# Values on every other partition, maxima turned by VectorE, and half tiles in the second layer's first pass

## The chip, the cores and the metric

The kernel runs on one core of a Trainium2 chip. The metric is device time in microseconds (us) from start to end of one execution; lower is better. A core has five engines that work side by side, each through its own list of instructions: TensorE (PE, matrix products), VectorE (DVE), ScalarE (ACT), GpSimd (POOL) and SyncE (SP, which here issues nearly all DMA transfers). They work on SBUF, a memory of 128 partitions (rows); TensorE writes its sums into PSUM, eight banks of 2 KB a partition (512 fp32 numbers). DRAM is reached by DMA only.

## The reference

Two layers on B = 2 sequences of T = 2048 tokens with D = 256 features, all fp32. Each layer normalizes x, runs an attention and a gate on the result, and adds their product.

```python
def attn0(x):                       # full attention, 16 heads of 16 features
    q, k, v = split(x @ w_qkv.T + b_qkv)
    p = softmax(q @ k.T / sqrt(256))
    return (p @ v) @ w_o.T + b_o + x
def attn1(x):                       # local attention: only keys with |i - j| <= 64
    q, k, v = x @ w_qkv + b_qkv
    p = softmax(q @ k.T * 16**-0.5 + band)
    return (p @ v) @ w_out + b_out
for attn, ffn in ((attn0, ffn0), (attn1, ffn1)):
    xn = layernorm(x)
    x = x + attn(xn) * silu(ffn(xn))
```

ffn0 mixes 8 experts of 64 features with a running sum over the sequence, ffn1 is a linear layer with 8 low-rank experts. The change doesn't touch them.

## The kernel before

Everything lies with features on partitions and tokens along the row (`x`, `xn`, `gt`: [128, 2, 2048] per sequence). The stages follow each other: weights and first norm; ffn0; `attention` for layer 0; second norm and ffn1; `attention` again with `local=True`.

**Heads in row groups.** `attention` keeps the queries and keys of four heads at a time in tiles `qs[.]`, `ks[.]`: head j of the group in partitions 32j to 32j+31 (`hp`, L548), of which 16 hold values. A matmul of one head uses 32 rows of the array, so four heads fill the four row groups. `keys_queries` (L473) projects and writes to the DRAM tensor `qd` [2, B, H, 32, T]; `fetch` (L581) brings 32 rows a head back. Rows 16 to 31 of `qd` were preset with ones (keys) and zeros (queries) by DMA (L304 to L311). Row 16 of the queries later gets minus the query's largest score, so that the product with the ones subtracts it. Two sets of `qs`, `ks` alternate.

**Items and steps.** An item is (sequence, group of four heads, block of 512 queries): 32 of them. A step of layer 0 is one block of 128 keys against the item's 512 queries (U = 16 steps an item); a step of layer 1 is two query blocks of 128 with the keys in their reach (U = 2). The main loop (L945) runs, per step s:

- `scores` (L596): TensorE computes two things. The **second pass** (`sk`) has keys as weights and queries as columns, for step s; ACT takes its exponential (L683), and in layer 1 GpSimd puts zeros outside the band (`affine_select`, L688). The **first pass** (`sq`) has queries as weights, for a step U + LEAD later; it serves only to find the maxima, by VectorE: in layer 0 a `tensor_reduce` (L679), in layer 1 `tensor_tensor_reduce` with a mask, eight a step (L674). Matmuls of both passes go out sorted by a number `when` (L666), which sends row groups 0, 1 through sk then sq and row groups 2, 3 the other way round.
- `weigh` (L733), DEL steps later: `acc` <- exponentials times values, one 32-column group per head (L747). The values `vs` hold 17 columns a head, the last all ones, so row 16 of each group of `acc` becomes the softmax's denominator. ACT copies `acc` to `av`.
- what `at(step, ...)` has booked for the step (L855 to L881): LEAD steps before an item begins, its maxima are turned from a column into a row; after the item, a chain with one hop or so a step divides and projects.

**Turning the maxima.** Layer 0 (`turn_max`, `fetch_max`): VectorE scales, SP writes element by element to DRAM (`md`), and three steps later reads it into `q` row 16. Layer 1 (`place_max`, L714): TensorE transposes (`pmx`, L720), ACT copies (L723), a DMA from ACT's queue puts the row in `q` (L726).

**The chain after an item** (L771 to L803), in layer 1 at hops 0, 1, 3, 4, 5, 7, 8: `away` writes `av` (128 x 512) to DRAM; `compact` reads the denominators back as [128, 16] (`dn`) and the values into `xn`; `invert` takes reciprocals; `write` puts them in DRAM; `spread` reads them broadcast over the head's rows (`recb`); `divide` multiplies (in layer 1 VectorE and GpSimd in turn); `project` (group 3 only) applies the output weights. The last four items of layer 1 go through TensorE instead (`last_there`, `last_back`).

**What sets the order.** A scheduler places instructions; those in `pin` keep their program order on their engine, so SP's transfers run in the order in which they are written. `values` (L526) projects the values, 17 blocks a sequence in layer 1, and VectorE or ACT copies them to `vs`, which GpSimd has set to ones before (L514).

Of the kernel before, what the change touches and what calls it, by code (L numbers as in the profile page):

```python
# [17 lines left out]
P = 128  # L18
# [6 lines left out]
HV = HD + 1  # L25
TB = 512
# [11 lines left out]
def two_layers(ctx: ExitStack, tc: tile.TileContext, a, out):  # L38
# [144 lines left out]
    def softmax8(pool, lg, groups, name):  # L183
# [12 lines left out]
        [2, B, H, HP, T], F32, name="qd"  # L196
# [3 lines left out]
    with tc.tile_pool(name="fw", bufs=1) as fw:  # L200
# [102 lines left out]

        zeros = fw.tile([P, TB], F32, name="zeros")  # L304
        nc.vector.memset(zeros, 0.0)
        for b in range(B):
            for i, t in ((0, ones), (1, zeros)):
                for half in range(NC):
                    nc.sync.dma_start(
                        out=qd[i, b, bass.ts(half, H // NC), HD:, :], in_=t[:, None, :].to_broadcast([P, NB, TB])  # L310
                    )  # L311
# [161 lines left out]
    def keys_queries(A, b, n, i, hf, bank, place):  # L473
        w, bias = ((A["k"], A["bk"]), (A["q"], A["bq"]))[i]
        ps = bank()
        for c in range(NC):
            nc.tensor.matmul(  # L477
                ps, w[:, c, bass.ts(hf, P)], xn[b][:, c, bass.ts(n, TB)], start=(c == 0), stop=(c == NC - 1)
            )
        sb = place()  # L480
        nc.scalar.activation(sb, ps, AF.Identity, bias=bias[:, hf : hf + 1])
        nc.sync.dma_start(out=qd[i, b, bass.ts(hf, H // NC), :HD, bass.ts(n, TB)], in_=sb)

    def attention(A, scale, local, final, start=None, projected=False):
# [16 lines left out]
        LEAD = 3 if local else 6  # L501
        DEL = 2 if local else 1
        with ExitStack() as st:
# [6 lines left out]
            ad = [dr.tile([NG, HP, TB], F32, name=f"ad{i}", tag=f"ad{i}") for i in range(3)]  # L510
            rd = [dr.tile([NG, TB], F32, name=f"rd{i}", tag=f"rd{i}") for i in range(3)]

            md = [dr.tile([NG * TT, P], F32, name=f"md{i}", tag=f"md{i}") for i in range(2)]
# [12 lines left out]
            def values(b, c, bank, copy):  # L526
                lo = c * P - PAD
                t0, t1 = max(lo, 0), min(lo + P, T)
                p0, p1 = t0 - lo, t1 - lo
                ps = bank()[:, :D]  # L530
                for dc in range(NC):
                    nc.tensor.matmul(  # L532
                        ps[p0:p1, :], xn[b][:, dc, t0:t1], A["v"][:, dc, :], start=(dc == 0), stop=(dc == NC - 1)
                    )
                copy(
                    vs[b][p0:p1, c, : H * HV].rearrange("p (h w) -> p h w", w=HV)[:, :, :HD],
                    ps[p0:p1, :].rearrange("p (h w) -> p h w", w=HD),
                )
# [10 lines left out]
            hp = [slice(j * HP, (j + 1) * HP) for j in range(NG)]  # L549
            ep = None if local else pool("ep", 8)  # L550
# [3 lines left out]
            if local:  # L554

                mask = mp.tile([P, 2 * P], F32, name="mask", bufs=1)
                nc.vector.memset(mask, 0.0)
                nc.gpsimd.affine_select(
                    out=mask, in_=mask, compare_op=ALU.is_ge, fill=MASKED, base=0,
# [3 lines left out]
                    out=mask, in_=mask, compare_op=ALU.is_ge, fill=MASKED, base=P,  # L563
                    pattern=[[-1, 2 * P]], channel_multiplier=1,
                )

# [14 lines left out]
            def fetch(bg, lo=0, hi=T):  # L581

                if bg >= B * NG:
                    return
                b, g = divmod(bg, NG)
                k0, k1 = max(lo - PAD, 0), (T if hi == T else hi - PAD)
                for i, t in ((1, qs[bg % 2]), (0, ks[bg % 2])):
                    to, s = (slice(lo, hi), slice(lo, hi)) if i else (slice(PAD + k0, PAD + k1), slice(k0, k1))
                    nc.sync.dma_start(out=t[:, to], in_=qd[i, b, bass.ts(g, NG), :, s].rearrange("h w t -> (h w) t"))
# [6 lines left out]
            def scores(second, first, es):  # L596
# [7 lines left out]
                if second:  # L604
# [3 lines left out]
                    if local:  # L608

                        qt = n * TT + 2 * u  # L610
                        segs = [
                            (P, 3 * P, bass.ts(qt + 1, P), bass.ds(qt * P, 2 * P)),
                            (0, P, bass.ts(qt, P), bass.ts(qt, P)),
                            (3 * P, 4 * P, bass.ts(qt + 2, P), bass.ts(qt + 1, P)),
                        ]
                    else:
                        segs = [(0, TB, bass.ts(u, P), bass.ts(n, TB))]
# [8 lines left out]
                    for j in range(NG):  # L626
# [6 lines left out]
                        when = 2 * (j // 2) if apart else 0  # L633
                        for lo, hi, ks_, qs_ in segs:
                            pieces.append((when, t[:, lo:hi], k[hp[j], ks_], q[hp[j], qs_]))
                            when += 2 * (hi - lo) / TB
                        tasks.append((es[j], t))
                pairs = []
                if first:
# [9 lines left out]
                    for pair in ((2, 3), (0, 1)):  # L649
                        sq = pmax.tile([P, 2, TB], F32, name="sq", tag="sq")  # L650
                        pairs.append((pair, sq))
                        for d, j in enumerate(pair):
                            when = (2, 2, 0, 0)[j] if apart else 0
                            if local:
                                for t in range(2):
                                    qt, lo, hi = reach(n1, u1, t)
                                    pieces.append((
                                        when + t, sq[:, d, t * 2 * P + lo : t * 2 * P + hi],
                                        q1[hp[j], bass.ts(qt, P)], k1[hp[j], qt * P + lo : qt * P + hi],
                                    ))  # L660
                            else:
                                t, kb = divmod(u1, NB)
                                pieces.append((
                                    when, sq[:, d], q1[hp[j], bass.ds(n1 * TB + t * P, P)], k1[hp[j], bass.ts(kb, TB)]
# [3 lines left out]
                for pair, sq in pairs:  # L668
                    if local:
                        for d, j in enumerate(pair):  # L670
                            for t in range(2):
                                qt, lo, hi = reach(n1, u1, t)
                                seen = mp.tile([P, 2 * P], F32, name="seen", tag="seen")
                                nc.vector.tensor_tensor_reduce(  # L674
                                    seen[:, lo:hi], sq[:, d, t * 2 * P + lo : t * 2 * P + hi], mask[:, lo:hi],
# [17 lines left out]
            def reach(n, u, t):  # L693

                qt = n * TT + 2 * u + t
                return qt, (PAD if qt == 0 else 0), (2 * P - PAD if qt == NT - 1 else 2 * P)

            pin = tc.keep_in_program_order

            def turn_max(i):  # L700

                mx, _ = part.pop(i)
                nmx = mp.tile([P, NG * TT], F32, name="nmx", tag="nmx")
                pin(nc.vector.tensor_scalar(nmx, mx.rearrange("p j t -> p (j t)"), -1.0, None, ALU.mult))
                pin(nc.sync.dma_start(out=md[i % 2].rearrange("j p -> p j"), in_=nmx))

            def fetch_max(i):

                pin(nc.sync.dma_start(
                    out=tiles(i)[0][HD:P:HP, bass.ts(items[i][2], TB)],  # L710
                    in_=md[i % 2].rearrange("(j t) p -> j (t p)", t=TT),
                ))

            def place_max(i):  # L714

                b, g, n = items[i]
                q = tiles(i)[0]
                mx, _ = part.pop(i)
                ps = pm.tile([NG * TT, P], F32, name="pmx", tag="m")
                nc.tensor.transpose(ps, mx.rearrange("p j t -> p (j t)"), ident)  # L720
                row = mp.tile([NG * TT, P], F32, name="row", tag="row", bufs=2 if local else 1)
                if local:
                    pin(nc.scalar.activation(row, ps, AF.Copy, scale=-1.0))  # L723
                else:
                    nc.vector.tensor_scalar(row, ps, -1.0, None, ALU.mult)
                pin((nc.scalar if local else nc.sync).dma_start(  # L726
                    out=q[HD:P:HP, bass.ts(n, TB)].rearrange("j (t c) -> j t c", c=P), in_=row
# [37 lines left out]

# [5 lines left out]
            def away(i):  # L771

                pin(nc.sync.dma_start(out=ad[i % 3].rearrange("j w f -> (j w) f"), in_=avs.pop(i)))

            def flat(d):

                return d.rearrange("j (r e) -> r j e", r=P // NG)

            def compact(i):

                divs[i] = op.tile([P, NG * TB // P], F32, name="dn", tag="dn", bufs=3)
                pin(nc.sync.dma_start(out=divs[i], in_=flat(ad[i % 3][:, HD, :])))
                pin(nc.sync.dma_start(out=together(*items[i]), in_=ad[i % 3][:, :HD, :].rearrange("j d f -> d j f")))
# [7 lines left out]
            def spread(i):  # L791
# [4 lines left out]
                pin(nc.sync.dma_start(out=divs[i], in_=rd[i % 3][None, :, :].to_broadcast([HD, NG, TB])))  # L796
# [8 lines left out]
            def last_there(i):  # L805
# [3 lines left out]
                for t in range(TT):  # L809
                    nc.tensor.transpose(ps[:, t].rearrange("p j w -> p (j w)"), av[:, bass.ts(t, P)], ident)  # L810
                rec = op.tile([P, TT, NG], F32, name="dn", tag="dn", bufs=3)
                o = divs[i] = op.tile([P, TT, HD, NG], F32, name="over", tag="recb", bufs=2)
                nc.vector.reciprocal(rec, ps[:, :, :, HD])
                nc.vector.tensor_tensor(
                    o.rearrange("p t d j -> p t j d"), ps[:, :, :, :HD],
                    rec[:, :, :, None].to_broadcast([P, TT, NG, HD]), ALU.mult,
                )

            def last_back(i):
# [3 lines left out]
                o = divs.pop(i).rearrange("p t d j -> p t (d j)")  # L823
# [35 lines left out]
            for i, (b, g, n) in enumerate(items):  # L859
                if local:  # L860
                    at(i * U - LEAD, place_max, i)
                else:
                    at(i * U - LEAD, turn_max, i)
                    at(i * U - LEAD + 3, fetch_max, i)
# [257 lines left out]
def _attn_arrays(l, wq, wk, wv, bq, bk, bv, wo_t, bo):  # L1122

    apart = lambda m: m.reshape(NG, NG, HD, -1).transpose(0, 2, 1, 3).reshape(m.shape)
# [5 lines left out]
        f"wo{l}": apart(np.asarray(wo_t).T),  # L1130
        f"bq{l}": cols(bq),
        f"bk{l}": cols(bk),
        f"bv{l}": cols(apart(np.asarray(bv))),
# [56 lines left out]
```

## Time and profile before

| | |
|---|---|
| median of 3 runs | 2535.94 us (2533.43 to 2537.54) |
| the profiled execution, its span | 2538.34 us, 2536.6 us |
| 0 to 470: weights, norm, ffn0 | PE busy 461.8 |
| 470 to 597: layer 0's projections and first steps | PE busy 124.7 |
| 597 to 2111: layer 0's attention, 512 steps | PE busy 1513.9 of 1514 |
| 2111 to 2225: norm and ffn1 | PE busy 110.0 of 114 |
| 2225 to 2292: layer 1's projections and first steps | PE busy 66.2 of 67 |
| 2292 to 2537: layer 1's attention, 64 steps and the end | PE busy 236.5 of 245 |

TensorE's granted clock is 0.999 over the span. In the rows of a stretch or of single instructions that follow, PE is the matmuls and PEld the loading of their weights, which runs beside them. A matmul row names its output and inputs, the tile of the array that it uses (32*128: 32 rows, 128 columns), and the columns that flow through it. Times are in us from the start of the span; the number before the engine is the duration.

### The profile page before, as it was taken

How to read it: one execution, taken by the hardware profiler on the slowest of the kernel's cores; microseconds unless marked ns; L12 is line 12 of the kernel's file. 1: busy time of each engine (PE TensorE's matmuls, PEld its weight loads, DVE VectorE, ACT ScalarE, POOL GpSimd, SP SyncE). 2: the span in 40 equal slices, each digit the busy share in tenths (PEclk: the TensorE clock that was granted, in tenths of full speed). 3: DMA queues.
4: the chain of work that ended last, by engine and by line, in shares of the span. 5: the costliest groups of instructions: out<-in, count | busy, mean ns of one | idle time of the engine just before them, and what ended most of it. 6: DMA issues, size and time to landing. Idle time of an engine off the chain costs nothing.

```text
span 2536.6 us, 47898 instructions
## 1 busy us (share of the span) xinstructions
PE 2513.1 (99%) x18896; PEld 1060.6 (42%) x18896; DVE 1686.2 (66%) x2747; ACT 1620.8 (64%) x3187; POOL 876.6 (35%) x827
## 2 busy tenths in 40 slices
PE   8999999999999999999999999999999999999999
PEld 6444444444333333333333333333333334457766
DVE  4143333157888888888777788788888765238986
ACT  5400000126888888888888888888888886227755
POOL 0000000102444444444444444444444420016887
PEclk9999999999999999999999999999999999999999
DMA  6131111230001001001001001001000002133552
GB/s 243 50 84 51 52 51 39 82 118 14 14 14 43 16 12 44 16 12 44 16 12 43 10 18 44 12 17 43 15 14 10 14 14 63 49 133 108 163 167 81
DMA packets 146353, 129.83 MB, mean 51 GB/s; under 512 B 93456, under 2 KB 97936, under 8 KB 143568
## 3 DMA queue, kind: packets, MB, share of 16 engines
q1 hardware_dynamic: 144256, 125.46, 16.5%
q8 instruction: 148, 2.42, 0.4%
q10 hardware_dynamic: 1872, 1.31, 0.2%
q14 instruction: 77, 0.63, 0.1%
HBM read 80.50 MB, written 45.97 MB: 50 GB/s over the span
## 4 chain that ended last, share of the span: by engine, by line
PE 79%; DMA 1%; ACT 0%; POOL 0%; DVE 0%; issue 0%; ACTq 0%; SPq 0%; POOLq 0%; DVEq 0%
PE sk L667 25%; PE acc L747 22%; PE sq L667 19%; PE pp L477 5%; PE pr L835 2%; PE pp L532 2%; PE po L1027 1%; PE pt L1023 1%; PE po L1035 1%; PE xb L113 0%; PE xb L138 0%; DMA k<-qd 0%; PE of L827 0%; DMA q<-qd 0%; POOL xn L688 0%
## 5 line engine op out<-in xcount | busy, mean ns | idle before, releaser
L679 DVE TENSOR_REDUCE part<-sq 128x2 f32<-128x1024 f32 x1024 | 1207.3, 1221 | 294.3 <-PE sq L667 284.7
L683 ACT ACTIVATE e<-sk 128x512 f32<-128x512 f32 x2048 | 1058.3, 603 | 217.2 <-PE sq L667 197.7
L667 PE MATMUL sk<-q,k 32*128 32x512 f32 (+2 forms) x5632 | 1135.8, 533 | 1.2 <-ACT xn L683 1.0
L667 PE MATMUL sq<-k,q 32*128 32x512 f32 (+2 forms) x5120 | 1129.1, 569 | 0.5 <-DVE part L679 0.5
L761 POOL TENSOR_TENSOR av<-av,more 128x512 f32<-128x512 f32 x459 | 581.4, 1267 | 936.3 <-ACT more L760 931.1
L667 PEld LDWEIGHTS sk<-q,k 32*128 32x128 f32 x5632 | 522.0, 184 | 604.1 <-ACT e L683 512.5
L747 PE MATMUL acc<-e,v 128*32 128x512 f32 x4096 | 546.7, 605 | 0.0
L667 PEld LDWEIGHTS sq<-k,q 32*128 32x128 f32 x5120 | 402.3, 183 | 22.3 <-DVE part L679 13.2
L760 ACT COPY more<-acc 128x512 f32<-128x512 f32 x459 | 268.7, 585 | 1.2 <-PE acc L747 1.0
L747 PEld LDWEIGHTS acc<-e,v 128*32 128x32 f32 x4096 | 81.8, 108 | 388.2 <-ACT e L683 367.8
L461 ACT ACTIVATE gt<-po 128x512 f32<-128x512 f32 x16 | 8.8, 594 | 321.1 <-PE po L457 321.1
L674 DVE CUSTOM_DVE_ANT_0 seen<-sq,mask 128x256 f32<-128x256 f32 (+1 forms) x512 | 176.2, 410 | 53.6 <-PE sq L667 49.2
L467 POOL TENSOR_TENSOR x<-x,up 128x512 f32<-128x512 f32 x16 | 23.1, 1461 | 450.1 <-DVE up L464 277.5
L448 DVE TENSOR_TENSOR xs<-we,px 128x512 f32<-128x512 f32 x64 | 43.9, 686 | 136.2 <-PE px L440 130.3
L688 POOL TENSOR_SCALAR_AFFINE_SELECT xn<-xn 128x512 f32<-128x512 f32 x172 | 106.2, 652 | 77.4 <-ACT xn L683 75.7
L440 PE MATMUL px<-xn,FV 128*128 128x512 f32 x256 | 121.2, 595 | 0.0
L444 PE MATMUL py<-cum,FW 128*128 128x512 f32 x256 | 120.5, 593 | 0.6 <-DVE cum L412 0.6
L424 PE MATMUL po<-pr,UO 128*128 128x512 f32 x256 | 119.0, 592 | 0.0
L683 ACT ACTIVATE xn<-sk 128x512 f32<-128x512 f32 x172 | 89.8, 602 | 41.1 <-PE sk L667 17.9
L450 DVE TENSOR_TENSOR pr<-xs,py 128x512 f32<-128x512 f32 x64 | 44.0, 687 | 64.8 <-PE py L444 64.6
L424 PEld LDWEIGHTS po<-pr,UO 128*128 128x128 f32 x256 | 48.6, 190 | 61.2 <-issue 61.0
L444 PEld LDWEIGHTS py<-cum,FW 128*128 128x128 f32 x256 | 48.4, 190 | 61.5 <-issue 59.8
(195 smaller groups left out, 1604.0 us busy)
## 6 DMA issues: line engine op xcount, KB each, us to landing
we<-wd SPq DMA_DIRECT2D x128, 128.0 KB
ad<-av SPq DMA_DIRECT2D x59, 256.0 KB
qd<-sb SPq DMA_DIRECT2D x48, 256.0 KB
k<-qd SPq DMA_DIRECT2D x10, 1024.0 KB
q<-qd SPq DMA_DIRECT2D x10, 1024.0 KB
xn<-ad SPq DMA_DIRECT2D x59, 128.0 KB
recb<-rd SPq DMA_DIRECT2D x59, 128.0 KB
q<-qd SPq DMA_DIRECT2D x12, 512.0 KB
```

The lines of the kernel that those rows point to most:

```text
L424: nc.tensor.matmul(po[oc], UO[:, ch, bass.ts(oc, P)], pr, start=(ch == 0), stop=False)
L440: nc.tensor.matmul(px, FV[:, c, bass.ts(ch, P)], xn[b][:, c, cols], start=(c == 0), stop=(c == NC - 1))
L444: nc.tensor.matmul(py, FW[:, c, bass.ts(ch, P)], cum[:, c, :], start=(c == 0), stop=(c == NC - 1))
L477: nc.tensor.matmul(ps, w[:, c, bass.ts(hf, P)], xn[b][:, c, bass.ts(n, TB)], start=(c == 0), stop=(c == NC - 1))
L667: nc.tensor.matmul(o, lhs, rhs, start=True, stop=True)
L674: nc.vector.tensor_tensor_reduce(seen[:, lo:hi], sq[:, d, t * 2 * P + lo : t * 2 * P + hi], mask[:, lo:hi], 1.0, LOWEST, ALU.add, ALU.max, ...
L679: nc.vector.tensor_reduce(pt[:, pair[0] : pair[1] + 1, t, kb], sq, AX.X, ALU.max)
L683: nc.scalar.activation(e, t, AF.Exp, scale=scale)
L688: nc.gpsimd.affine_select(out=e[:, :, c, :], in_=e[:, :, c, :], compare_op=ALU.is_ge, fill=0.0, base=0, pattern=[[0, 4], [sign, P]], chann ...
L747: nc.tensor.matmul(acc[hp[j], o : o + hi - lo], vs[b][:, kt, vcols(g, j)], es[j][:, lo:hi], start=(r == 0), stop=(r == len(parts) - 1), sk ...
L760: nc.scalar.copy(more, acc)
L761: nc.gpsimd.tensor_tensor(avs[i], avs[i], more, ALU.add)
```

## The change

Five things change, all in `attention` and what feeds it.

1. **Layout.** Values sit in the even partitions of each group of 32, the odd ones hold 1 (keys) or 0 (queries), set once per attention in SBUF by VectorE; `qd` loses its 16 constant rows and the DMAs that preset them. Minus the maximum goes to partition 31. The first pass uses 31 rows (`hq`), without it. The columns of `vs` are interleaved with ones to match, and the denominator is row 15 of each group.
2. **Turning.** Both layers use `turn_max` and `fetch_max`; VectorE scales into every other column of a zeroed tile and transposes 128x32 in blocks of 32; 16 even partitions are written to `md`. LEAD is 6 in both layers. `place_max` is gone.
3. **Half tiles, layer 1.** A first-pass matmul has 64 queries as weights and 192 keys as columns instead of 128 and 256; the two halves lie in different partitions of the same `sq`. The second pass has 64 keys as weights. The mask becomes [128, 3, 192], one form each for inner blocks, the first and the last.
4. **The chain after an item.** `away` writes only the four denominator rows; `compact` reads them as [32, 64] and takes the values straight from `av`; `spread`'s broadcast has the heads outermost.
5. With heads in their natural order in `xn`, the output weights and value bias are no longer permuted on the host.

```diff
-        [2, B, H, HP, T], F32, name="qd"
+        [2, B, H, HD, T], F32, name="qd"
...
-        zeros = fw.tile([P, TB], F32, name="zeros")
-        nc.vector.memset(zeros, 0.0)
-        for b in range(B):
-            for i, t in ((0, ones), (1, zeros)):
-                for half in range(NC):
-                    nc.sync.dma_start(
-                        out=qd[i, b, bass.ts(half, H // NC), HD:, :], in_=t[:, None, :].to_broadcast([P, NB, TB])
-                    )
...
-        LEAD = 3 if local else 6
+        LEAD = 6
+        DE = 64
...
+            for k, q in zip(ks, qs):
+                nc.vector.memset(k, 1.0)
+                nc.vector.memset(q, 0.0)
...
-                nc.sync.dma_start(out=t[:, to], in_=qd[i, b, bass.ts(g, NG), :, s].rearrange("h w t -> (h w) t"))
+                nc.sync.dma_start(out=t[::2, to], in_=qd[i, b, bass.ts(g, NG), :, s].rearrange("h w t -> (h w) t"))
...
-                            (P, 3 * P, bass.ts(qt + 1, P), bass.ds(qt * P, 2 * P)),
-                            (0, P, bass.ts(qt, P), bass.ts(qt, P)),
-                            (3 * P, 4 * P, bass.ts(qt + 2, P), bass.ts(qt + 1, P)),
+                            (sub, lo, hi, bass.ds((qt + kt) * P + sub * PAD, PAD), bass.ds(q0, hi - lo))
+                            for kt, lo, hi, q0 in (
+                                (1, P, 3 * P, qt * P), (0, 0, P, qt * P), (2, 3 * P, 4 * P, (qt + 1) * P)
+                            )
+                            for sub in range(2)
...
-                                    qt, lo, hi = reach(n1, u1, t)
-                                    pieces.append((
-                                        when + t, sq[:, d, t * 2 * P + lo : t * 2 * P + hi],
-                                        q1[hp[j], bass.ts(qt, P)], k1[hp[j], qt * P + lo : qt * P + hi],
-                                    ))
+                                    for sub in range(2):
+                                        q0 = (n1 * TT + 2 * u1 + t) * P + sub * PAD
+                                        pieces.append((
+                                            when + t * RC / (2 * P), sq[halves[sub], d, bass.ts(t, RC)],
+                                            q1[hq[j], bass.ds(q0, PAD)], k1[hq[j], bass.ds(q0, RC)],
+                                        ))
...
+                m = nmx[i % 2]
+                pin(nc.vector.tensor_scalar(m[:, :, 0], mx.rearrange("p j t -> p (j t)"), -1.0, None, ALU.mult))
+                turned = mp.tile([P, HP], F32, name="tmx", tag="tmx")
+                pin(nc.vector.transpose(turned, m.rearrange("p i e -> p (i e)")))
+                pin(nc.sync.dma_start(out=md[i % 2].rearrange("i s r -> s i r"), in_=turned[::2]))
...
-                pin(nc.sync.dma_start(out=ad[i % 3].rearrange("j w f -> (j w) f"), in_=avs.pop(i)))
+                pin(nc.sync.dma_start(out=ad[i % 3], in_=avs[i][DEN::HP]))
...
-                pin(nc.sync.dma_start(out=divs[i], in_=flat(ad[i % 3][:, HD, :])))
-                pin(nc.sync.dma_start(out=together(*items[i]), in_=ad[i % 3][:, :HD, :].rearrange("j d f -> d j f")))
+                pin(nc.sync.dma_start(out=divs[i], in_=flat(ad[i % 3])))
+                pin(nc.sync.dma_start(out=together(*items[i]), in_=avs.pop(i)[::2]))
...
-                pin(nc.sync.dma_start(out=divs[i], in_=rd[i % 3][None, :, :].to_broadcast([HD, NG, TB])))
+                pin(nc.sync.dma_start(out=divs[i], in_=rd[i % 3][:, None, :].to_broadcast([NG, HD, TB])))
...
-                if local:
-                    at(i * U - LEAD, place_max, i)
-                else:
-                    at(i * U - LEAD, turn_max, i)
-                    at(i * U - LEAD + 3, fetch_max, i)
+                at(i * U - LEAD, turn_max, i)
+                at(i * U - LEAD + 3, fetch_max, i)
```

## The prediction

> **What bounds the kernel now.** I read the page's sums first, then the table by stretches of time, then the instructions of some steps in order of time, since the sum only says that TensorE is always busy.
>
> ```profile
> span 2536.6 us, 47898 instructions
> ...
> PE 2513.1 (99%) x18896; PEld 1060.6 (42%) x18896; DVE 1686.2 (66%) x2747; ACT 1620.8 (64%) x3187; POOL 876.6 (35%) x827
> ```
>
> ```profile
> 597.00:2111.00 1514.00, 1513.88 (x12184) 514.20 (x12184) 1205.00 (x1147) 1295.42 (x2541) 636.96 (x503) 1.00 0.08 21
> ...
> 2225.00:2292.00 67.00, 66.17 (x320) 41.61 (x322) 22.38 (x102) 18.60 (x37) 9.63 (x10) 1.00 0.38 126
> ...
> 2300.00:2366.00 66.00, 65.60 (x1314) 52.82 (x1310) 59.07 (x334) 48.62 (x112) 53.74 (x86) 1.00 0.49 151
> ```
>
> (Columns: stretch, its length, then busy time of PE, PEld, DVE, ACT, POOL, clock, DMA share, GB/s.) The first layer's attention (597 to 2111) is all TensorE, the others at 80, 86 and 42%; DMA is idle. In the second layer (from 2225) TensorE is full too, but VectorE is at 89% and GpSimd at 81%: little has to fall off TensorE before another engine decides.
>
> One step of the second layer, in order of time:
>
> ```profile
> 2373.66 1.08 PE L747 MATMUL acc<-elast,v 128*32 128x128 f32 x24
> 2374.67 0.28 PE L720 MATMUL pmx<-ident,mx 128*16 128x128 f32 x1
> 2374.88 0.62 PE L667 MATMUL sk<-q,k 32*128 32x256 f32 x2
> ...
> 2376.94 1.08 PE L747 MATMUL acc<-xn,v 128*32 128x128 f32 x24
> 2377.95 0.48 PE L667 MATMUL sk<-q,k 32*128 32x256 f32 x2
> ...
> 2380.07 1.08 PE L747 MATMUL acc<-xn,v 128*32 128x128 f32 x24
> ```
>
> From acc to acc 3.28 us where a maximum is turned by TensorE (L720, once per item of two steps), 3.13 where not; over the plain steps the first kind is mostly 3.39, the mean 3.26. Of 3.13, acc holds 1.01 and the scores of both passes 2.12.
>
> **The first pass in half tiles.** How fast the four row groups run:
>
> ```profile
> 2331.96 0.48 PE L667 MATMUL sk<-q,k 32*128 32x256 f32 x2
> 2331.98 0.48 PE L667 MATMUL sq<-k,q 32*128 32x256 f32 x2
> 2332.28 0.38 PE L667 MATMUL sk<-q,k 32*128 32x256 f32 x2
> ...
> 2332.50 0.28 PE L667 MATMUL sk<-q,k 32*128 32x128 f32 x2
> ```
>
> Each f32 matmul is recorded as two passes. Four row groups start within 0.02 us, and a pass of 256 columns hands over after 0.22 (2332.28 to 2332.50), so 0.84 ns a column; the very first waits 0.10 longer for its 128 weight columns (2331.96 to 2332.28). Two row groups bear sk then sq: 512 columns in two passes each, 2 x 0.43 plus two first loads of 0.10 and small waits, 2.02, and 0.1 to drain: the 2.12 above. Afterwards sq has 2 x 192 columns a row group, 0.64 instead of 0.85; sk keeps its columns, but in twice as many matmuls, for 64 keys each. If the two column halves of a row group run side by side, as the four column groups of acc do (24 in 1.08), scores take 2.12 - 0.21 - 2 x 0.05 (half the weight columns) - 0.04 (128-column pieces no longer held up by their loads) = 1.77, and a plain step 2.78. Bounds: 32*64 tiles stand in no row here. Below, 1.67 if all waits go; above, halves one after the other: 2 x 0.85 + 2 x 0.64 + 0.3 = 3.3. I take 1.77, nearest to acc's row.
>
> **A rule against it.** The Trainium skill (TensorE: Matmul & The Clock Gate, section "Wait — 56ns, not 53.3ns?") says that matmuls start no closer than about 25 ns, however short. A step's scores are 40 matmuls, 80 passes: by the rule at least 2.0, so a step of 3.0 to 3.1. The rows above have four starts in 0.02 us in different tiles, so I follow the row; by the rule the gain is a third (2529 below).
>
> **The turned maximum.** L720 goes: 3.39 - 3.13 = 0.26 an item, 0.13 a step. ACT loses its copy (0.26) and the issue behind it (0.53). In their place VectorE gets a 128x16 scaling (0.17, the row of the first layer) and a 128x32 transpose, in no row; between 0.1 and 0.3, taken at 0.17 as the scaling. SP gets two more issues an item at 0.53.
>
> **What the other engines then need a step.** VectorE's maxima, start to start:
>
> ```profile
> 2249.20 0.36 DVE L674 CUSTOM_DVE_ANT_0 seen<-sq,mask 128x192 f32<-128x192 f32 x1 [8.19 <-PE sq L667]
> ...
> 2249.48 0.42 DVE L674 CUSTOM_DVE_ANT_0 seen<-sq,mask 128x256 f32<-128x256 f32 x1
> ...
> 2249.83 0.35 DVE L674 CUSTOM_DVE_ANT_0 seen<-sq,mask 128x192 f32<-128x192 f32 x1
> ```
>
> 0.28 for 192 columns, 0.35 for 256: eight a step fall from 2.76 to 2.22. To it per step: half of scaling and transpose (0.17), half a reciprocal, which grows from 16 to 64 elements a partition (0.25 for 16 and 0.35 for 32 give about 0.57 for 64: 0.28), a quarter of a division (0.84): 2.88. GpSimd: 83 selections in 51.2 us in the stretch 2300 to 2366, 0.62 each, four a step, and a quarter of 1.27: 2.79. ACT: 4 x 0.52 + 0.40 = 2.5. So TensorE 2.78, VectorE 2.88, GpSimd 2.79: I take **2.90**, VectorE's plus a little.
>
> **SP and the transfers.** An item's issues on SP are now md, q<-md, ad, dn, xn, rd, recb and half of two fetches, some 4.4 us of 5.8. md waits for the transpose; recb, dn and xn of other items queue behind, and GpSimd's division waits for recb, its selections behind it. There are two steps between recb and its division, three between q<-md and its matmuls: hidden; without this cover, 1 us late an item is 30 us. recb now has an outer size of 4. By the skill (DMA: Bandwidth & Descriptors, section "Rules for kernel authors") such a transfer stays on four of 16 engines: 32 KB each instead of 8, by its 27 GiB/s an estimated 0.85 us longer, still inside two steps. Fetches are halved, which relieves this:
>
> ```profile
> 2383.52 5.28 DMA k<-qd
> ```
>
> Behind such fetches ACT's small row transfer came late; TensorE stood still 0.3 near 2390 and 1.2 near 2469. I take 1.0 back. The earlier first pass leaves a fetched second half of k three steps (8.7 us) instead of six, more than these 5.28. av is freed one step later (its denominators go to DRAM, its values are read directly), with three buffers: three steps of slack. Ones and zeros (8 MB) are no longer written to DRAM: TensorE is full while they are (462 of 470 us), nothing. Strided copies of v, weights in another order, 31 rows instead of 32 (still one row group): nothing. In the first layer the memsets of k and q fall under 29 us of projections, and VectorE's scaling was there already; bound there: 2 us either way.
>
> **The memsets before the second layer's values.**
>
> ```profile
> 1.27 0.48 DVE L302 MEMSET ones<- 128x512 f32 x1
> ...
> 2225.32 15.23 PE L532 MATMUL pp<-wv,xn 128*64 128x256 f32 x68 [0.69 <-ACT gt L1039]
> ...
> 2228.95 2.43 DVE L535 COPY v<-pp 64x256 f32<-64x256 f32 x6 [2.89 <-POOL v L515]
> ```
>
> 0.48 for 512 and 0.11 for 64 give 0.83 ns an element: 7.3 us for two k and two q. In the new order of VectorE they stand in front of the copies of v, which then begin near 2233.5 instead of 2228.95. TensorE fills six banks at 0.9 and stops at 2230.7: +3.0 (0 if the memory is free earlier; 5 if GpSimd's memset of v, at the same time, and these hold each other up).
>
> **The sum.** The 64 steps' acc groups run from 2298.8 to 2519.3: 48 plain steps, 8 with a projection (4.97 each), 8 at the end.
> - plain: 48 x (3.26 - 2.90) = -17.3
> - with projection, where TensorE alone decides: 8 x (0.35 + 0.13, less 0.10 for coupling) = -3.0
> - end: -1.0; fetches: -1.0
> - memsets +3.0; three more steps of first pass alone before the loop (0.75 each, against five that shrink by 0.2): +1.2
>
> -18.1: the execution profiled (2538.3, its span 2536.6) would become 2520.2; the median of the runs shown, 2535.9, lies 2.4 below it: **2518**.
>
> **Rivals.**
> 1. Another engine takes over sooner (VectorE's semaphores, GpSimd behind recb, SP at 4.4 of 5.8, or the 25 ns rule): a step of 3.1 gives 48 x 0.16 + 3 + 2 - 4.2 = 8.5, 2527; of 3.2, 2532. For it: 89% and 81% above. Against: each has slack by its rows.
> 2. Slower, one mechanism: TensorE's supply of instructions. A step goes from 128 loads and passes to 208. Sustained, the trace shows 3.13 us / 128 = 24 ns each and in bursts 3 to 7; it can't say which is the limit. It decides from 15 ns (208 x 15 = 3.1, where the extra 4.2 are no longer won back). At 20 ns a step is 4.2: 56 x 0.9 + 4 = 54, 2590.
> 3. The halves of a row group don't overlap: 3.3 - 2.12 - 0.13 = +1.05 a step, 64 x 1.05 + 4 = 71, 2607. Against: acc's column groups do.
>
> **Chances.** Forecast 2505 to 2526: 0.60. Rival 1 (2526 to 2541): 0.23, two thirds of it faster. Rival 2: 0.10. Rival 3: 0.07. What a measurement tells from no change is 0.2%, 5 us: faster (under 2530.9) 0.60 + 0.15 = 0.75, same 0.08, slower 0.17. The range runs from 2504 (all three engines at 2.78, no stall at the memsets: 18.1 + 6 + 3, and the first layer's 2) to 2548, which leaves out most of rivals 2 and 3; the likeliest case alone is 2505 to 2526.
>
> **What would show it.** Right: acc groups 2.8 to 3.0 apart in plain steps, no TensorE transposes at 128x128 between them; 32x64 passes of 192 columns handing over after 0.16; VectorE above 95% busy there; 597 to 2111 still 1514 long; about 3 us of standstill in the values before the second attention. Wrong: steps at 3.1 or more with VectorE or GpSimd waiting for recb or dn; passes of the halves starting 0.16 or more apart in one row group (rival 3); TensorE idle with "issue" as the reason (rival 2); a first-layer step other than 2.93.

## The result and the profile after

The changed kernel takes 2541.25 us (median of 12 runs, 2536.61 to 2544.02), the kernel before 2536.15 (12 runs, 2532.11 to 2539.51): a ratio of 1.0020, 95% interval 1.0011 to 1.0028. It is slower by 0.2%, where 2518 was forecast; the forecast's own range ended at 2526, the wide one, 2504 to 2548, holds the time on the wrong side of no change. The profiled execution took 2539.14 us, its span is 2537.4.

The page of the changed kernel (sums, and the row of the queue that brings TensorE's instructions):

```profile
span 2537.4 us, 53134 instructions
...
PE 2498.5 (98%) x21424; PEld 1042.1 (41%) x21424; DVE 1717.1 (68%) x2862; ACT 1617.0 (64%) x3155; POOL 877.5 (35%) x827
...
q8 instruction: 168, 2.75, 0.5%
```

The same stretches as before, with the same columns (PE, PEld, DVE, ACT, POOL, clock, DMA share, GB/s):

```profile
597.00:2111.00 1514.00, 1511.00 (x12177) 514.24 (x12173) 1221.62 (x1188) 1295.09 (x2541) 638.38 (x504) 1.00 0.04 12
...
2225.00:2292.00 67.00, 62.31 (x432) 37.26 (x432) 29.46 (x153) 17.53 (x32) 3.74 (x9) 0.97 0.25 88
...
2300.00:2366.00 66.00, 62.62 (x2179) 48.47 (x2168) 59.93 (x364) 48.95 (x105) 55.34 (x88) 1.00 0.27 82
```

In layer 1's steps TensorE fell from 65.60 to 62.62 busy of 66, and nobody took its place: VectorE is at 91%, GpSimd at 84%. TensorE stands still, in a stretch where it was always busy. Set side by side by the starts of the stages' first matmuls, the two profiled executions differ so:

| stretch | before | after | difference |
|---|---|---|---|
| start to layer 0's first acc | 599.65 | 595.14 | -4.5 |
| layer 0's acc groups | 1510.86 | 1508.00 | -2.9 |
| to the last matmul of ffn1 | 113.53 | 115.02 | +1.5 |
| layer 1: values, first value to last | 14.86 | 20.98 | +6.1 |
| last value to first acc | 58.60 | 59.18 | +0.6 |
| layer 1: 64 acc groups, first start to last | 220.52 | 220.52 | 0.0 |

The first row is chance: in the fourteen profiles of this study the first transpose starts at 13.2 to 13.6 or at 10.9 to 11.4, whatever the version, and the way from there to the first acc takes 582.7, some 584.2, or 585.8 to 586.3. Without this row the two profiled executions differ by 5.3 us, as the medians do (5.1). The third row is not explained: it lies between 113.5 and 117.2 in the fourteen. What remains is 2.9 won, 6.7 lost, and the 22 us that layer 1's steps were to give, which are not there.

**A step.** An undisturbed one, in order of time:

```profile
2315.02 1.07 PE L747 MATMUL acc<-elast,v 128*32 128x128 f32 x24
...
2316.03 0.45 PE L681 MATMUL sk<-q,k 32*64 32x256 f32 x4
...
2316.05 0.56 PE L681 MATMUL sq<-k,q 31*64 31x192 f32 x8
...
2317.56 0.33 PE L681 MATMUL sk<-q,k 32*64 32x128 f32 x4
...
2317.99 1.50 PE L747 MATMUL acc<-xn,v 128*32 128x128 f32 x24
```

From acc to acc 2.97, the shortest plain step there is and the commonest; before it was 3.26 in the mean. (The last acc row is long because it already holds the next standstill.) But the mean over the 34 plain steps ahead of the projections is 3.28. The difference, 10.5 us in sum, is nearly all of one kind:

```profile
2385.58 0.43 PE L681 MATMUL sk<-q,k 32*64 32x128 f32 x8
...
2387.86 0.39 PE L681 MATMUL sq<-k,q 31*64 31x192 f32 x4 [1.85 <-issue]
```

"issue" says that no semaphore was late. With TensorE's records (loads, passes and a few of its sequencer) numbered from 0 at the first in the trace, the standstills fall on one and the same place: number 32705, 33729, 34241, 35009, 35265, 36033 and so on, each 193 more than a multiple of 256, called "the 193rd" below. Of the 10.5 us, 9.3 lie there. The packets of queue q8 above have 16 KB, 168 of them for 43056 records, so one packet for 256. In every such standstill a packet has ended 1.2 to 1.7 us before TensorE goes on. The one for this standstill (2385.43 to 2386.30) began when the data ahead of it were through. The DMA view's rows by queue, the first for 2381 to 2385.4, the others for 2385.4 to 2387.9 (packets, MB, share of 16 engines):

```profile
q1 hardware_dynamic: 393, 0.78, 56.0%
...
q1 hardware_dynamic: 95, 0.03, 6.4%
q8 instruction: 1, 0.02, 2.2%
```

For 4.4 us the 16 engines were 56% busy with fetched keys, queries and values and no instructions came. Packets otherwise begin about 3.7 us apart here (3.45, 3.68 from 2300.6 on); this one came 5.7 after the last.

**The memsets.** Layer 1's values in order of time, and two rows of the table by stretches (the standstill, and what follows it):

```profile
2224.67 1.87 DVE L509 MEMSET k<- 128x2176 f32 x1 [0.40 <-issue]
...
2226.92 1.76 DVE L510 MEMSET q<- 128x2048 f32 x1 [0.38 <-issue]
...
2228.72 2.54 DVE L533 COPY v<-pp 64x256 f32<-64x256 f32 x7
...
2229.21 11.60 PE L529 MATMUL pp<-wv,xn 128*128 128x256 f32 x44 [4.18 <-DVE v L533]
```

```profile
2229.30:2233.20 3.90, 3.90 (x11) 3.13 (x12) 2.39 (x7) 0.00 (x0) 0.00 (x0) 0.56 0.56 174
2224.90:2229.10 4.20, 0.13 (x1) 0.00 (x0) 3.79 (x3) 0.00 (x0) 3.84 (x9) 1.00 0.65 189
```

The copies of v wait for four memsets (of k and q, two of each; two are shown), TensorE waits 4.2 us for the copies, and then its granted clock is 0.56 for 3.9 us: passes of 256 columns stand 0.43 apart instead of 0.22. That is the 6.1 us of the table.

### The profile page after: what moved, and what is told of

It is laid out like the page before. It is cut to its first block, busy times and chain, and to the rows that moved or that the text cites. A ratio compares the mean times of both kernels' runs of the same rounds, so it can differ in the third digit from the quotient of the medians.

```text
span 2537.4 us, 53134 instructions
## 1 busy us (share of the span) xinstructions
PE 2498.5 (98%) x21424; PEld 1042.1 (41%) x21424; DVE 1717.1 (68%) x2862; ACT 1617.0 (64%) x3155; POOL 877.5 (35%) x827
## 4 chain that ended last, share of the span: by engine, by line
PE 77%; issue 1%; POOL 1%; DVE 1%; ACT 1%; DMA 0%; SPq 0%; POOLq 0%; ACTq 0%; DVEq 0%
PE sk L681 24%; PE acc L747 22%; PE sq L681 19%; PE pp L469 4%; PE pr L833 2%; PE pp L529 2%; PE po L1022 1%; PE pt L1018 1%; PE po L1030 1%; POOL xn L702 0%; POOL elast L702 0%; PE xb L139 0%; PE xb L114 0%; ACT xn L697 0%; POOL xn L801 0%
## 5 line engine op out<-in xcount | busy, mean ns | idle before, releaser
L681 PE MATMUL sq<-k,q 31*128 31x512 f32 (+1 forms) x6144 | 1112.7, 520 | 3.5 <-issue 2.8
L681 PEld LDWEIGHTS sk<-q,k 32*128 32x128 f32 (+1 forms) x7168 | 501.8, 161 | 613.7 <-ACT e L697 518.5
L681 PEld LDWEIGHTS sq<-k,q 31*128 31x128 f32 (+1 forms) x6144 | 385.0, 166 | 29.2 <-issue 14.3
L688 DVE CUSTOM_DVE_ANT_0 seen<-sq,mask 128x192 f32<-128x192 f32 x512 | 146.8, 350 | 45.2 <-PE sq L681 44.2
```

Source lines behind the costliest of these rows:

```text
L681: nc.tensor.matmul(o, lhs, rhs, start=True, stop=True)
L688: nc.vector.tensor_tensor_reduce(seen, sq[:, d, bass.ts(t, RC)], mask[:, (qt == 0) + 2 * (qt == NT - 1), :], 1.0, LOWEST, ALU.add, ALU.max ...
```

## The experiments

Chips differ: the kernel before takes 2536 us in two of the series and 2541 in three. So versions are compared by their ratio to the kernel before on the same chip, and where possible with a version of the same series. The theory: layer 1's steps at 208 loads and passes outrun the supply of instructions (**supply**), and the memsets cost 6 us. The rival: transfers of data that TensorE's operands wait for.

**The changed kernel again.** No edit.

> The changed kernel once more, on the chip of this series, so that the versions below stand against it and not only against the kernel before. Both theories: 0.2% above the kernel before. A second profile tells which of its standstills are the same each time: by the supply theory all long ones of layer 1's steps fall on the same instruction of a block of 256, and fewer of them recur at the same step; by the rival (data transfers) they have no such place.

2543.97 us, ratio 1.0013 (1.0003 to 1.0023). The long standstills are again on the 193rd, 21 of them above 0.2 us; of the fifteen above 0.4 us nine stand in the first profile too (numbers 31425, 32705, 33729, 34241, 35265, 36033, 37057, 37313 and 41153). The supply theory as written wanted fewer to recur at the same step than that; it had not reckoned that the data ahead of a packet are the same each time.

**The second pass in whole tiles.**

```diff
-                            (sub, lo, hi, bass.ds((qt + kt) * P + sub * PAD, PAD), bass.ds(q0, hi - lo))
+                            (None, lo, hi, bass.ts(qt + kt, P), bass.ds(q0, hi - lo))
...
-                            for sub in range(2)
```

> The changed kernel, but the second pass of layer 1 in whole tiles (128 keys as weights); the first pass stays in half tiles. A step then has 160 loads and passes on TensorE instead of 208. Supply theory: TensorE's instructions come in blocks of 256 by DMA, and at 208 in 2.97 us a block comes too late now and then (some 13 us in sum over layer 1's steps, each time at the same place in the block). With 160 these standstills are gone: step 2.9 to 3.1 throughout, 2527 to 2533 us. Rival, the halves of the second pass are what brought the step to 2.97 and the standstills come from transfers of data: step 3.2, standstills remain, 2541 or more.

2626.58 us (four runs), ratio 1.0346 (1.0329 to 1.0362). No standstill on the 193rd, as the theory has it, but every step takes 4.91, far from what both expected (2.9 to 3.1 and 3.2). TensorE's rows of one step:

```profile
2349.36 0.70 PE L680 MATMUL sk<-q,k 32*128 32x256 f32 x4
2349.99 0.88 PE L680 MATMUL sq<-k,q 31*64 31x192 f32 x16
2350.80 0.73 PE L680 MATMUL sk<-q,k 32*128 32x128 f32 x12
2351.46 0.55 PE L680 MATMUL sq<-k,q 31*64 31x192 f32 x8
2351.94 0.49 PE L680 MATMUL sk<-q,k 32*128 32x128 f32 x4
```

Tiles of the two shapes never run together: each group begins about when the one before is through (0.07 ahead of its modelled end), though they use different row groups. In the changed kernel sk and sq (32*64 and 31*64) start 0.02 apart.

**The same with the two passes one after the other.**

```diff
-                        when = [1.5 * (j // 2) if apart and local else 2 * (j // 2) if apart else 0] * 2
+                        when = [-9.0 if apart and local else 2 * (j // 2) if apart else 0] * 2
```

> As second_whole (keys in whole tiles, queries in halves, a step of 4.91 us), but all matmuls of the second pass come ahead of those of the first, so that a step changes the tile shape 3 times instead of 8. Theory: a change of shape makes TensorE wait until all matmuls of the other shape are through, also in other row groups, some 0.2 us each, and row groups stand empty meanwhile: now 1.06 + 0.84 + 1.01 = 2.9 us a step, up to 3.7 where PSUM banks come free too late. Rival, it is the mixture of column widths in one row group: 4.9 stays.

2558.55 us (two runs), ratio 1.0074 (1.0057 to 1.0092), a step of 3.52 throughout. So it is the change of shape, and fewer changes win 1.39 us a step. The size was wrong in one term, the second pass: 1.66 instead of 1.06 (45.13 to 46.79 in these rows), the other two as worked out.

```profile
2344.13 1.08 PE L746 MATMUL acc<-xn,v 128*32 128x128 f32 x24
...
2345.13 1.73 PE L680 MATMUL sk<-q,k 32*128 32x256 f32 x24
...
2346.79 0.93 PE L680 MATMUL sq<-k,q 31*64 31x192 f32 x32
...
2347.65 1.08 PE L746 MATMUL acc<-xn,v 128*32 128x128 f32 x24
```

**Both passes in whole tiles.** The matmuls, the mask and the maxima of layer 1 as before the change, all else as changed.

```diff
-                                    for sub in range(2):
-                                        q0 = (n1 * TT + 2 * u1 + t) * P + sub * PAD
...
+                                    qt, lo, hi = reach(n1, u1, t)
...
```

> The changed kernel, but both passes of layer 1 in whole tiles (as before the change): layout, turning by VectorE and the chain after an item stay as changed; 128 loads and passes a step. Supply theory: no standstill at a fixed place in the block; step 3.13 throughout (the step of before without a transpose), memsets still cost 6: 2531 to 2536 us. Rival, the standstills come from the new turning and transfers: they stay, 2541 or more.

2547.9 us, ratio 1.0023 (1.0013 to 1.0034). The standstills on the 193rd are gone, yet the steps average 3.35, as VectorE is now the bound: it has no room left (90 us of layer 1's steps), and the first pass's loads wait for its maxima 13 times.

```profile
2310.00:2400.00 90.00, 89.43 (x1738) 68.60 (x1734) 89.02 (x474) 64.58 (x136) 71.42 (x113) 1.00 0.28 83
```

The time is the rival's (2541 or more), but not by its standstills; both had left out that eight maxima of 256 columns (2.76) and the turning together fill VectorE. It shows that the half tiles are worth little beside this layout, as they leave VectorE's bound for the supply's: the 64 acc groups take 221.8 us here and 220.5 to 224.1 in the four profiles with half tiles and the same SP queue. Whether it is nothing stays open: writes_back below, with half tiles and of the same series, is 6.5 us shorter in the median, though in the two profiles only some 3 us of difference show, all ahead of the first acc.

**The memsets on GpSimd.**

```diff
+            on = nc.gpsimd if local else nc.vector
+            if local:
+                tc.keep_in_program_order(on.memset(vs[0], 1.0))
             for k, q in zip(ks, qs):
-                nc.vector.memset(k, 1.0)
-                nc.vector.memset(q, 0.0)
...
+                tc.keep_in_program_order(on.memset(k, 1.0)) if local else on.memset(k, 1.0)
+                tc.keep_in_program_order(on.memset(q, 0.0)) if local else on.memset(q, 0.0)
...
```

> The changed kernel, but in layer 1 the memsets of k and q are GpSimd's, between those of the two v tiles, instead of VectorE's. Theory: the copies of the values start some 5 us sooner, TensorE doesn't stop for 4.2 us and doesn't run at half rate for 4 us behind it; 6 us less, 2535 us. Rival, the wait only moves (to the fetches of k and q that need the memsets, or VectorE and GpSimd hold each other up): 2539 to 2541.

2536.28 us, ratio 0.9982 (0.9975 to 0.9988), 5.1 us below writes_back of the same series. The values take 14.86 us again, as before the change, at full clock:

```profile
2220.10:2235.40 15.30, 15.23 (x68) 12.25 (x68) 7.29 (x17) 0.00 (x0) 15.30 (x11) 1.00 0.42 132
```

**The output transfers later.** The memsets are GpSimd's here too. In layer 1 SP issues the output of a block two to four steps after its projection.

```diff
...
+                    if final and i < len(items) - 1:
+                        at(end + DEL + hops[-1] + (4 if i < len(items) - NB else 2), send, i)
```

> The changed kernel with GpSimd's memsets (as in memsets_pool), and the output transfers of layer 1 put two to four steps later in SP's queue. Theory: q<-md stands behind an output transfer that waits for GpSimd's addition, which costs the step near 2456 some 2.7 us; it no longer does: 6 + 2.5 us less than the changed kernel. Rival, the row is late for another reason (its own way through DRAM): 6 us less only, and the 2.7 us stay.

2534.34 us, ratio 0.9972 (0.9962 to 0.9981), 9.6 us below the changed kernel of the same series; on a second chip:

> mem_out once more, side by side with no_fetch on one chip, since the two stood on different chips so far, where the kernel before itself differs by 5 us. Both theories: between 0.9970 and 0.9990 of the kernel before.

2532.99, 0.9969 (0.9958 to 0.9980), a hair below what was expected. This row of the changed kernel's waits (2410 to 2522; total, times, longest) has no counterpart any more:

```profile
PE sk L681 <- DMA q<-md: 2.9, 2, 2.7
```

The maximum's row had stood on SP behind outputs, of which one had waited 4.1 us for GpSimd. The step with this wait took 5.73 and takes 3.63 and 3.64 in the two profiles of mem_out. mem_out is faster than both kernels, by 0.3 and 0.4%.

**Fetches in quarters, and a transfer on ACT's queue.**

```diff
-                if local and n == NB // 2 - 1:
-                    at(end, fetch, b * NG + g + 2, 0, T // 2)
...
+                if local:
+                    at(end, fetch, b * NG + g + 2, n * TB, (n + 1) * TB)
...
```

> As mem_out, and the fetches of keys and queries in layer 1 go out in quarters, one after each item, instead of in halves after every second. Theory: a block of instructions comes late because its transfer begins behind a burst of fetched data (2.4 us late near 2385); smaller bursts hold it up less, and the standstills on the 193rd instruction fall from some 13 us to 8 or 9: 4 us less than mem_out. Rival, the blocks are late with or without such bursts: the same as mem_out.

2534.96 us, ratio 0.9975 (0.9965 to 0.9984), the same as mem_out, which is the rival's time. The standstills fell from 14.3 to 11.8 us, less than the theory wanted (8 or 9), and rows of maxima came late for 3.8 us in three waits, for SP has one issue more an item. Next, the denominators go to DRAM from ACT's queue as well:

```diff
-                pin(nc.sync.dma_start(out=ad[i % 3], in_=avs[i][DEN::HP]))
+                pin((nc.scalar if local else nc.sync).dma_start(out=ad[i % 3], in_=avs[i][DEN::HP]))
```

> As mem_out_quart (fetches in quarters), and the transfer of the denominators to DRAM goes out from ACT's queue, behind ACT's own copy of them, instead of SP's. Theory: with quarters the standstills on the 193rd instruction fell, but SP's queue had one issue an item more and the maxima's rows came late (3.8 us in three waits); with an issue taken off SP again these go: 3 to 4 us less than mem_out_quart, 0.9960 of the kernel before. Rival: ACT's issues (0.5 us an item) delay its exponentials and TensorE waits for these instead: no gain.

2536.46 us, ratio 1.0001 (0.9993 to 1.0009): the rival was right.

```profile
PE acc L750 <- ACT xn L700: 10.1, 7, 2.2
```

**The ones and zeros written again.**

```diff
...
+                        out=qx[i, b, bass.ts(half, H // NC)], in_=t[:, None, :].to_broadcast([P, NB, TB])
...
```

> The changed kernel, with the 8 MB of ones and zeros that it no longer writes to DRAM written again, at the same place in the program, to a tensor that nobody reads. Theory: these writes hold up the loads at the start, the first norm's matmuls come 2.9 us later as before the change, and the whole is 2.5 to 3 us longer: 2544. Rival, the 2.9 us are chance of one execution: 2541.

2541.41 us, ratio 1.0002 (0.9994 to 1.0010), no longer than the changed kernel: the rival was right, the late start is chance. That the ratio lies below the changed kernel's in two other series (1.0020, 1.0013) is not explained; ratios of different series are thus compared to no better than 0.2%, 5 us.

**Without the fetches.** mem_out, but keys and queries of layer 1 are fetched for two of the eight groups of heads only and used again for the others: this kernel leaves out a part of the computation.

```diff
-                if bg >= B * NG:
+                if bg >= B * NG or local and bg > 1:
```

> As mem_out, but in layer 1 keys and queries are fetched only for the first two groups of heads and used again for the others (this part of the computation is left out). Theory: the fetches' bursts are what the blocks of instructions stand behind; the standstills on the 193rd instruction fall from 12.5 us to 3 or less, steps of 2.97 nearly throughout: 8 to 10 us less than mem_out. Rival: the round trip of a block is too slow at 208 instructions a step even without these bursts (by its own 1.1 us of transfer, 1.4 us behind it, and the broadcasts on few engines): most of the 12.5 us stay.

2526.64 us, ratio 0.9965 (0.9952 to 0.9978), on another chip than mem_out. On one chip:

> no_fetch (keys and queries of layer 1 fetched for two of the eight groups only, that part of the computation left out) beside mem_out on the same chip. Theory: the difference that the two profiles show, 10 us, holds for the medians too, at least 6 us: the blocks of instructions stand behind the fetches. Rival: the profiled execution of no_fetch, the fastest of its five, was a lucky one, and the medians differ by 3 us or less; then most of what TensorE waits for its instructions stays without the fetches.

2529.7 us, ratio 0.9952 (0.9941 to 0.9964) against 2532.99 for mem_out: 3.3 us less. The standstills are 5.2 and 9.0 us in the two profiles, against 14.3 and 14.0. Both profiled executions of no_fetch were the fastest of theirs. So the bursts make up a part, between 3 and 9 us; some standstills stay without them, nearer to the rival than to the theory. What holds those up (a packet's own 1 us and the 1.2 to 1.7 us behind it, or the broadcasts) was not told apart.

The standstills of all versions: sum over layer 1's attention of the distances between the 192nd and the 193rd start of each block of 256 (undisturbed 0.02 each), and the shortest of the plain steps.

```
version         loads and passes a step   shortest step   sum on the 193rd, us
before                   128                  2.98               0.5
both_whole               128                  3.00               0.6
second_whole             160                  4.91               1.1
grouped                  160                  3.52               0.9
after                    208                  2.97              13.3
again                    208                  2.97              15.3
memsets_pool             208                  2.97              15.2
writes_back              208                  2.97              15.5
mem_out                  208                  2.97              14.3, 14.0
mem_out_quart            208                  2.97              11.8
away_act                 208                  2.95               6.3
no_fetch                 208                  2.97               5.2, 9.0
```

At 208 in 2.97 us a block lasts 3.66 us, at 160 in 3.52 it lasts 5.6, at 128 in 3.26 6.5. Where TensorE waits for ACT besides (away_act), the supply catches up.

## Why the prediction was wrong

1. **What bounds the kernel, and the first layer.** Right, but for 2.9 us: layer 0's attention got shorter, where "TensorE is full" was read as no effect. Before, six of its 511 steps took 0.2 to 1.2 us longer than the same steps after it. In five of them TensorE's instructions were late here too: a packet of q8 came 17.5 to 18.4 us after the last one instead of 15.6, and ended 0.5 to 1.2 us before the slow step. It began 7.3 to 8.1 us after the element-by-element write of the maxima (2048 numbers, each a packet of 4 bytes), and no fetch of keys or queries ran. After the change, with maxima in rows, the same packets come after 15.0 to 16.0. No run changed this write alone, other packets as late cost nothing, and the sixth step shows no such sign.
2. **First pass in half tiles, 1.77.** Measured 1.96 (2.97 less 1.01). The column halves do run side by side, and passes of 192 columns hand over after 0.16. Mis-sized was mostly the drain: I had 0.1 between scores and acc; the last sk pass starts at 2317.62, its 128 columns hand over after some 0.11 (at 0.84 ns each), and acc starts at 2317.99, 0.26 later. Before the change 0.28 to 0.33 lay between the last start and acc, now 0.37. That tiles of different shape don't run together shows at large in second_whole.
3. **The rule against it.** By the rule of 25 ns 80 passes needed 2.0 us; their starts lie within 1.60, so 20 ns each: it doesn't hold across tiles.
4. **The other engines, 2.88 for VectorE.** 90.35 us busy in the 100 from 2310, in which some 30 steps lie, make 3.0 a step: the scaling of the maxima took 0.16 to 0.58, once 2.02, instead of 0.17, the transpose 0.21. VectorE is thus as full as TensorE where neither is disturbed, and the step of 2.90 became 2.97, 48 x 0.07 = 3.4 in the sum.
5. **The step that failed: "I take 2.90".** It has TensorE's time, VectorE's, GpSimd's and nothing for bringing the instructions. Rival 2 named the supply, but as a price for each instruction with a bound at 15 ns. Undisturbed steps run at 2.97 / 208 = 14.3 ns, just short of it; the loss comes in blocks, 0.2 to 2.1 us at a time, 13.3 us in sum. This is most of the 22 us; with 3.4 of point 4, 2.7 of point 6 and 2.0 of point 8 it makes 21.4. That it comes with the rate of instructions is shown: at 128 and 160 a step, in steps of 3.3 us and more, it is gone. What makes a packet late was settled in part only (no_fetch).
6. **SP: "hidden".** The row of the maximum was late once, for 2.7 us, behind an output transfer: I had listed SP's issues of an item, but not the output transfers and the wait that they bring into the queue. In the two runs of mem_out the step is 2.1 shorter. The broadcast was right: in layer 0 recb takes 2.8 to 3.2 us from its issue to its last packet instead of 1.9 to 2.1, closed by four packets of 4 bytes instead of 16, near the estimated 0.85 for four engines; in layer 1 VectorE waited for it three times, 2.7 us in sum.
7. **The memsets, 3.0.** The mechanism was right, the size half: 4.2 us of standstill, and 1.9 more at half clock. The four memsets took 7.3 us as worked out; left out were the 0.4 us for which VectorE stood idle before each of them. The Trainium skill (TensorE: Matmul & The Clock Gate, section "What's actually happening") has the half rate after some 3.4 us of idleness; my 3.0 stayed under it, the real 4.2 did not.
8. **Prelude and projections.** +1.2 was +0.6; a projection step fell from 4.98 to 4.86, 1.0 us for eight instead of 3.0.

## What to carry to other kernels

Count the instructions of a stage, not only its engine time: when TensorE works off a fetched block of instructions faster than the next can come past the data transfers, smaller tiles buy little. Tiles of 32*128 and 31*64 did not overlap in TensorE, so shrink both passes or neither, and set those of one shape together. When an engine's work moves to another, look at what stands in that engine's queue once per stage, such as a memset or an output transfer, not only at its load per step.

## What had not been expected of the hardware

- TensorE's instructions arrive in packets of 16 KB, one for 256 loads and passes, on the DMA engines that carry the data; after a standstill TensorE went on 1.2 to 1.7 us after a packet's end.
- A DMA of 2048 single numbers held up such a packet by some 2 us, 7 to 8 us after its issue (layer 0 before the change; seen in the trace, not tried by a run).
- Matmuls of 32*128 and 31*64 tiles in different row groups run one after the other: 4.91 us a step with the shapes mixed, 3.52 grouped, 2.97 with one shape in both passes.
- The start of the kernel has two courses, 2.5 us apart, whatever the version.
